# Last grouped FFN of a six-layer transformer kernel: its tokens in three parts, rows sent one token tile per round, some shared-expert work placed between the expert tiles

## The chip, the cores and the metric

The kernel runs on one core of one Trainium2 chip. The metric is device microseconds of one execution, lower is better; a profile of one execution shows where the time goes. The engines are named as in the profile: PE (matrix products; PEld is its weight load), DVE (vector), ACT (scalar), POOL (GpSimd, which also issues the indirect DMAs that scatter and gather rows), SP (which issues the plain DMAs).

## The reference

A residual stream x of 8 x 512 = 4096 tokens by 256 goes through six layers. Only the last one is rebuilt by the change, and its form is that of the fourth:

```python
x = x + 0.5 * _L0_ffn_ref(_layernorm(x), ...)      # 8 experts, expert picks tokens
x = x + _L0_attn_ref(_layernorm(x), ...)           # 16 heads of 16
x = x + 0.5 * _L0_ffn_ref(_layernorm(x), ...)
x = x + 0.5 * _L1_ffn_ref(_layernorm(x), ...)      # grouped FFN, first time
x = x + _L1_attn_ref(_layernorm(x), ...)           # 16 heads of 64
x = x + 0.5 * _L1_ffn_ref(_layernorm(x), ...)      # grouped FFN, last time

def _L1_ffn_ref(x, gate_w, w1, w2, w3, ws1, ws2, ws3):
    scores = softmax(xt @ gate_w.T)                # 16 experts in 4 groups
    # best 2 groups by their largest score, then the best 4 experts in them
    h1 = einsum('td,edi->tei', xt, w1); h3 = einsum('td,edi->tei', xt, w3)
    y = einsum('tei,eid,te->td', silu(h1) * h3, w2, c)   # c: the 4 weights, else 0
    z = silu(xt @ ws1) * (xt @ ws3) @ ws2                # shared expert, all tokens
    return y + z
```

All of it is in float32. A token tile is 128 tokens; there are 32 of them (TT), four to a group (QT).

## The kernel before

**How the grouped FFN is computed** (class Grouped, L1324). Each token goes to 4 of 16 experts. `routing` (L1401) computes for a part of the tokens which experts they choose and, from a running count, at which row of a list of slots each of the four copies belongs. `send` (L1380) scatters the normalised row of one token tile to its four slots in DRAM (`slots_d`): four indirect DMAs of 128 rows each, issued by POOL, at most four in flight. The list has 144 slot tiles of 128 rows, each belonging to one expert. `tile_steps` (L1758) then runs a software pipeline over the slot tiles: in `step(i)` the tile i is transposed (`turn`, tile names tpx, xT), tile i-1 goes through the expert's first products and the silu (`hide`, hs, sgs, as), tile i-3 is turned back (`back`, tpa, aT), and tile i-4 goes through the second product (`give`, yps) and, up to four tiles at a time, to DRAM (`ys_d`). `load` fetches up to four slot tiles (xs) and waits for all sends of the parts up to its own. `collect` (L1593) brings the results back: `gather` (L1562) is one indirect DMA by POOL (yg, 8 buffers), and two token tiles later `add` (L1585) multiplies by the weight and adds into x on DVE. The shared expert is cut into units (`shared`, L1712): per group of four token tiles two "hidden" units (8 products each, tile names hp, sg, at) and four "outputs" units (two products each, yp). `Pump` (L1864) runs such units, each one's DVE part after the next one's PE part.

**Parts.** The tokens are sent in parts so that slot tiles that are already full can be computed before all tokens are routed. `Grouped.__init__` works out which slot tiles are certainly full after each part (`closed`) and after how many tiles in the order of computing a part's results can be gathered (`ready`). The first grouped FFN has parts of (8, 8, 8, 8) token tiles, the last one (20, 12). For (20, 12) this gives closed = 0, 65 and ready = 96, 144.

**The first grouped FFN** (`ffn1_before`, L1889) routes and sends one part after another; `route_and_send` (L1701) has the routing call a function at its end that issues all sends of the part at once.

**The attention ahead of the last FFN** (`_attn1`, L1036) has 64 rounds n (8 sequences by 8 chunks of two heads), each in two halves g. `Front` (L1953) does for the 20 token tiles of part 0 the layer norm, the logits (`units`) and the routing during the attention, and sends them one tile per half in the last 20 halves, with a normalisation of one tile on POOL ahead of each four sends.

**The last grouped FFN** (`ffn1_after`, L2009) loads weights, prepares and routes part 1 (12 tiles), and then runs 148 rounds of `step(i)`. Each round advances the routing of part 1 by two pieces; the routing hands out its 48 sends at once in round 14. From round `begin` = 96 + 6 = 102 on, each round issues one or two gathers. After the loop all 48 shared units are pumped, with the rest of the gathers between them; `done` stores a token tile when both its last expert row and its shared output are added.

**What sets the order.** The code is emitted under a manual schedule, so each engine runs its instructions in the order in which the functions above are called; waits come from data and buffers, and from the dependencies that `send`, `gather` and `load` add by hand. POOL's queue in the last FFN holds only the 48 sends and then the 128 gathers; SP's holds weight loads, xs loads, ys stores and the stores of the output.

Of the kernel before, what the change touches and what calls it, by code (L numbers as in the profile page):

```python
# [9 lines left out]
F32 = mybir.dt.float32  # L10
# [51 lines left out]
class Kernel:  # L62
# [973 lines left out]
    def _attn1(self, ctx, weights, beside, after):  # L1036
# [171 lines left out]

        known = []
        steps = after.routing(0, front.lg, front.pool, row_psum, lambda: known.append(True))  # L1210
        groups = after.parts[0] // QT

# [5 lines left out]
        for first, tiles, n in ((3 * QT, 2 * QT, 10), (5 * QT, 3 * QT, 25)):  # L1218
            for t in range(0, tiles, 2):
                own[n] = moments(pool, stats, first + t)  # L1220
                n += 1
            own[n] = lambda first=first, tiles=tiles: self.ln_finish(pool, stats, first, tiles)

        begin = NC * groups + 2
        for t in range(0, after.parts[0], 2):
            own[33 + t // 2] = moments(front.pool, after.stats, t)
        assert len(own) == 4 + 6 + 2 + after.parts[0] // 2 and max(own) == begin
        last = own[begin]
        own[begin] = lambda: (last(), self.ln_finish(front.pool, after.stats, 0, after.parts[0]))

        E = mybir.EngineType
        with tc.manual_schedule(engines={E.PE, E.DVE, E.Activation, E.Pool}):
# [9 lines left out]
            for n in range(N):  # L1242
                b, c = divmod(n, NC)
                if c == 0:
                    coming = prepare(b + 1) if b + 1 < B else [[]] * NC
                if n + 2 < N:
                    fill += heads(n + 2)
                fill += coming[c]
                if 1 <= n - begin <= groups:
                    fill += front.units(n - begin - 1, row_psum)  # L1250

                def rest():

                    if beside:
                        beside.pop(0)()

                def ahead():

                    if n > begin + groups:
                        advance(steps, 1)  # L1260

                for half in range(2):
                    g = 2 * n + half
                    if g + 1 < 2 * N:
                        exps, divide = scores(g + 1)
                    if half == 0 and tail:
                        tail.pop(0)()
                    t = g - 2 * N + after.parts[0]
                    if t >= 0:
                        assert known  # L1270
                        front.send(t)
                    turn(n, 2 * half)
                    more = g + 1 < 2 * N
                    if more:
                        exps(1)
                    if half == 0 and tail:
                        tail.pop(0)()
                    ahead()
                    if fill:
                        fill.pop(0)()  # L1280
                    if more:
                        divide(0)
                    rest()
                    turn(n, 2 * half + 1)
                    ahead()
                    for _ in range(len(fill) if half else max(0, len(fill) - 3) // 2):
                        fill.pop(0)()
                    if more:
                        divide(1)
                    rest()  # L1290
                    ahead()
                if n in own:
                    own[n]()
                tail = products(n)
                if b > 0 and c < 2:
                    fill += project(b - 1)[2 * c : 2 * c + 2]
# [27 lines left out]
class Grouped:  # L1324
# [6 lines left out]
    def __init__(self, k, n, parts):  # L1331
# [40 lines left out]
        self.stored = []  # L1372

    def rows(self, engine, out, t):
        mv, rstd = self.stats
        engine.tensor_scalar(
            out, self.k.x[:, t, :], mv[:, t, 0:1], rstd[:, t : t + 1], ALU.subtract, ALU.mult
        )

    def send(self, h, t, row):  # L1380

# [3 lines left out]
        for r in range(TOPK):  # L1385
# [10 lines left out]
            tc.declare_no_dep(inst, group=f"read{self.n}", reason="rows of other tiles")  # L1396
            tc.add_to_no_dep_group(f"slots{self.n}", inst)
            self.sent.append(inst)
            self.of_part[h].append(inst)
# [208 lines left out]
    def enter(self, ctx):  # L1608
# [3 lines left out]
        self.work = ctx.enter_context(tc.tile_pool(name=f"f1w_{n}", bufs=2, reuse_waits="tile"))  # L1612
        self.route = ctx.enter_context(tc.tile_pool(name=f"f1r_{n}", bufs=1, reuse_waits="tile"))
        self.psum = ctx.enter_context(tc.tile_pool(name=f"f1p_{n}", bufs=1, space=PSUM, reuse_waits="tile"))
# [56 lines left out]
    def back(self, g):  # L1671
# [6 lines left out]
        if h not in self.lg:  # L1678
            self.lg[h] = self.route.tile([P, self.parts[h], E1], F32, name="lg", bufs=2)
        at = g * QT - self.base[h]  # L1680
        nc.vector.tensor_copy(self.lg[h][:, at : at + QT, :], lg)

    def prepare(self, h):
# [3 lines left out]
        for t in range(a, b, 2):  # L1687
            k.ln_moments(self.route, self.stats, t, 2)
            yield
        k.ln_finish(self.route, self.stats, a, b - a)  # L1690
        yield
# [8 lines left out]

    def route_and_send(self, h):  # L1701
        def send():
            for t in range(self.parts[h]):
                self.send(h, t, self.xn[:, self.base[h] + t, :])

        return self.routing(h, self.lg[h], self.route, self.row_psum, send)

# [4 lines left out]
    def shared(self, g):  # L1712
# [4 lines left out]
        def hidden(s):  # L1717
# [15 lines left out]
            def dve():  # L1733
                at = self.acts[g, s] = self.work.tile([P, CH], F32, name="at", bufs=4)
                nc.vector.tensor_tensor(at, hs[2], hs[1], ALU.mult)
            return pe, dve

        def outputs(i):
# [12 lines left out]
            def dve():  # L1751
                nc.vector.scalar_tensor_tensor(x[:, t, :], box[0], 0.5, x[:, t, :], ALU.mult, ALU.add)
            return pe, dve
# [4 lines left out]
    def tile_steps(self):  # L1758
# [46 lines left out]
        def hide(j):  # L1805
# [9 lines left out]
            st[j]["a"] = work.tile([P, P], F32, name="as", bufs=4)  # L1815
            nc.vector.tensor_tensor(st[j]["a"], sg, hp[:, 1, :], ALU.mult)  # L1816

# [71 lines left out]
def ffn1_before(k, f):  # L1889
# [4 lines left out]
    with ExitStack() as ctx, k.tc.manual_schedule(engines={E.PE, E.DVE, E.Activation, E.Pool, E.SP}):  # L1894
# [13 lines left out]
        for h in range(2):  # L1908

            pair = groups[2 * h : 2 * h + 2]  # L1910
            pump.feed(pair[0][0] + pair[1][0] + pair[0][1] + pair[1][1])
            routing, preparing, more = f.route_and_send(h), f.prepare(h + 1), True
            while more:

                sent = bool(f.of_part[h])
                more = advance(routing, 3)
                if sent:
                    more = advance(preparing, 2) or more
                pump.run(1)
        pump.flush()  # L1920
        load(0)
        for h in (2, 3):
            one, two = groups[2 * h], groups[2 * h + 1]
            pump.feed(one[0] + two[0] + one[1] + two[1])
            routing, preparing, more = f.route_and_send(h), f.prepare(3) if h == 2 else iter(()), True
            while at < f.closed[h - 1] or more:
# [6 lines left out]
                more = advance(preparing, 1) or more  # L1933
                pump.flush()
        while pump.units or pump.pending:
            pump.run(1)
# [16 lines left out]
class Front:  # L1953


    def __init__(self, k, f, ctx):
# [3 lines left out]
        k.nc.sync.dma_start(out=self.gw, in_=k.w["gate_wT"].rearrange("(c p) e -> p c e", p=P))  # L1960
        self.lg = self.pool.tile([P, f.parts[0], E1], F32, name="chosen")
        self.xn = {}
# [8 lines left out]

    def units(self, g, row_psum):

        k, nc = self.k, self.k.nc
        xn = self.normal(g * QT, QT)
        xnT = self.pool.tile([P, DC, CH], F32, name="xnT")
# [19 lines left out]
        def back():  # L1996
            lg = row_psum(QT * E1).rearrange("p (t e) -> p t e", e=E1)
            for i in range(QT):
                nc.tensor.transpose(lg[:, i, :], box[0][:, i * P : i * P + P], k.ident[0:E1, 0:E1])
            nc.vector.tensor_copy(self.lg[:, g * QT : g * QT + QT, :], lg)  # L2000

        box = []
        return [column(c) for c in range(DC)] + [logits, back]

    def send(self, t):
        self.f.send(0, t, self.normal(t, 1)[:, t % QT, :])


def ffn1_after(k, f, out):  # L2009
# [4 lines left out]
    with ExitStack() as ctx, k.tc.manual_schedule(engines={E.PE, E.DVE, E.Activation, E.Pool, E.SP}):  # L2014
        f.enter(ctx)
        a = f.parts[0]
        load, step, total = f.tile_steps()
        f.expert_weights()
        load(0)
        f.shared_weights()  # L2020
        part = f.prepare(1)
        while advance(part, 1):
            pass
        part = f.route_and_send(1)
        left = {t: 2 for t in range(TT)}
# [6 lines left out]
        coming = f.collect(done)  # L2032
        begin = f.ready[0] + 6
        rest, more = list(range(a // QT)), True
        for i in range(total):
            step(i)
            more = more and advance(part, 2)
            if not more and rest and i % 4 == 0:
                f.normal(rest.pop(0))
            if i >= begin:  # L2040
                for _ in range(1 + i % 2):
                    coming.pop(0)()

# [16 lines left out]
        for one, two in zip(groups, groups[1:]):  # L2060
            pump.feed(two[0] + one[1])
        pump.feed(groups[-1][1])
        at = 0
        while pump.units or pump.pending:
            pump.run(1)
# [8 lines left out]
def tile_kernel(tc, w, out):  # L2074
    with ExitStack() as ctx:
# [12 lines left out]
        weights, coming = ffn1_before(k, one)  # L2088
        two = Grouped(k, 1, (20, 12))
        k.attn1(weights, coming, two)  # L2090
# [74 lines left out]
```

## Time and profile before

| | us |
|---|---|
| median of 3 runs (4102.02 to 4124.71) | 4116.74 |
| the profiled execution | 4112.13 |
| its span, first to last instruction | 4110.4 |
| ... first grouped FFN, about | 1847 to 2373 |
| ... attention ahead of the last FFN, about | 2383 to 3627 |
| ... last grouped FFN | 3627 to 4110 |
| PE busy, of the span | 3641.7 (89%) |
| DVE / ACT / POOL busy | 2113.4 / 1475.7 / 1204.1 |

The profile is one execution. Windows of the span show for each engine how long it was busy and at what share of full speed PE's clock was granted. A timeline line gives start, duration, engine, line, operation, and in brackets how long the engine sat idle before it and who ended that; "remote" and "another core or an unknown queue" stand where the profile finds no releaser, "issue" where the engine waited for nothing that the profile shows. An indirect DMA's line shows the time that POOL spends on issuing it, not its transfer.

### The profile page before, as it was taken

The page shows a single profiled execution, that of the slowest core. Times are in us where ns is not written, and L with a number is a line of the kernel's source. Part 1 is how long each engine was busy: PE and PEld are TensorE (multiplying, and loading weights), DVE is VectorE, ACT ScalarE, POOL GpSimd, SP SyncE. Part 2 cuts the span into 40 slices and gives each one's busy share as a digit, 9 for nine tenths or more (in the row PEclk, how much of TensorE's full clock was granted, in tenths as well). Part 3 has the DMA queues.
Part 4 walks back from the last instruction along what each step waited for, and adds up shares of the span by engine and source line. Part 5 has one row for each costly group of instructions (what it writes and reads, how often), then busy time and mean ns, then how long its engine had stood idle before and what let it go on. Part 6 is the DMA issues. An engine that isn't in the chain of part 4 may idle for free.

```text
span 4110.4 us, 51131 instructions
## 1 busy us (share of the span) xinstructions
PE 3641.7 (89%) x17088; PEld 2139.1 (52%) x17088; DVE 2113.4 (51%) x5628; ACT 1475.7 (36%) x3387; POOL 1204.1 (29%) x1098
## 2 busy tenths in 40 slices
PE   4999979999995799986668989999999999986978
PEld 2666643444442566653346844555555444554754
DVE  6222126666665321214432578777777678652354
ACT  3222223444443222221224435445444434432421
POOL 2433333433412333323351512200000205513165
PEclk7999987999987899997788999999999999987998
DMA  5333247311003233324134711000000001143453
GB/s 194 68 78 74 57 108 241 114 27 27 14 19 104 55 67 71 80 51 134 58 131 147 250 31 32 27 10 1 1 1 1 1 1 48 56 147 127 158 168 105
DMA packets 262994, 316.62 MB, mean 77 GB/s; under 512 B 31697, under 2 KB 232785, under 8 KB 262481
## 3 DMA queue, kind: packets, MB, share of 16 engines
q1 hardware_dynamic: 213584, 212.12, 16.2%
q0 software_dynamic: 49152, 101.24, 10.1%
q8 instruction: 142, 2.33, 0.2%
q14 instruction: 116, 0.94, 0.1%
HBM read 157.81 MB, written 147.06 MB: 74 GB/s over the span
## 4 chain that ended last, share of the span: by engine, by line
PE 52%; issue 11%; DVE 8%; POOL 4%; another core or an unknown queue 4%; ACT 3%; DMA 1%; POOLq 0%; ACTq 0%; DVEq 0%
PE hs L1808 6%; PE zp L1175 5%; PE sp L1127 5%; PE tp L1161 5%; PE pq L1102 4%; PE yps L1828 3%; PE yp L1194 3%; PE pv L1082 3%; PE hp L1724 3%; PE st L874 3%; POOL acc_d L538 2%; PE sp L833 2%; PE tpx L1790 2%; PE pp L726 2%
## 5 line engine op out<-in xcount | busy, mean ns | idle before, releaser
L1139 ACT ACTIVATE ex<-sp,nmax 128x512 f32<-128x512 f32 x512 | 344.8, 685 | 469.5 <-DVE nmax L1132 454.9
L531 PE MATMUL op<-w,hid 128*128 128x256 f32 x2048 | 456.2, 380 | 0.0
L518 PE MATMUL hp<-exT,w 128*128 128x512 f32 x1024 | 450.1, 598 | 0.0
L1568 POOL DMA_INDIRECT yg<-ys_d,slot x256 | 266.4, 1040 | 573.6 <-DMA ys_d<-ys 210.4
L531 PEld LDWEIGHTS op<-w,hid 128*128 128x128 f32 x2048 | 384.9, 190 | 57.0 <-issue 7.7
L538 POOL DMA_INDIRECT acc_d<-ob,idx x128 | 207.0, 1617 | 571.9 <-ACT ob L537 571.9
L1808 PE MATMUL hs<-w_sb,xT 128*128 (+1 forms) x1152 | 321.7, 404 | 50.9 <-ACT xT L1792 25.7
L536 DVE TENSOR_TENSOR ob<-op,b 128x256 f32<-128x256 f32 x128 | 54.4, 425 | 542.8 <-PE op L531 465.7
L1161 PEld LDWEIGHTS tp<-ident,ex 128*128 128x128 f32 x2048 | 228.7, 141 | 182.6 <-issue 107.7
L518 PEld LDWEIGHTS hp<-exT,w 128*128 128x128 f32 x1024 | 193.9, 192 | 233.1 <-issue 231.8
L1132 DVE TENSOR_REDUCE nmax<-sp 128x2 f32<-128x1024 f32 x256 | 300.3, 1214 | 17.5 <-PE sp L1127 16.2
L522 ACT ACTIVATE hid<-hp,b 128x512 f32<-128x512 f32 x256 | 175.9, 687 | 324.1 <-PE hp L518 304.5
L841 DVE CUSTOM_DVE_ANT_0 junk<-sp,mask 128x256 f32<-128x256 f32 (+3 forms) x512 | 249.5, 487 | 81.6 <-PE sp L833 58.4
L1161 PE MATMUL tp<-ident,ex 128*128 128x128 f32 x2048 | 279.3, 279 | 13.5 <-DVE eT L204 12.5
L1386 POOL DMA_INDIRECT slots_d<-wide,slot x176 | 173.8, 988 | 337.7 <-DVE lane L1523 231.7
L1127 PE MATMUL sp<-qk,qk 64*128 64x512 f32 x1024 | 257.4, 621 | 2.2 <-ACT ex L1139 2.2
L1808 PEld LDWEIGHTS hs<-w_sb,xT 128*128 128x128 f32 x1152 | 209.2, 202 | 80.2 <-ACT xT L1792 30.4
L1149 DVE TENSOR_SCALAR ex<-ex,rec 128x512 f32<-128x512 f32 x512 | 245.7, 522 | 8.8
L1102 PE MATMUL pq<-xnT,wide 128*128 128x512 f32 x512 | 241.7, 596 | 5.5 <-ACT qk L1108 5.5
L1816 DVE TENSOR_TENSOR as<-sgs,hs 128x128 f32<-128x128 f32 x288 | 82.4, 286 | 303.9 <-ACT sgs L1814 245.1
L1175 PE MATMUL zp<-eT,v 128*64 128x512 f32 x1024 | 234.9, 599 | 0.0
L889 ACT ACTIVATE ex<-st 128x768 f32<-128x768 f32 (+1 forms) x192 | 168.5, 882 | 160.1 <-DVE st L887 157.4
(346 smaller groups left out, 5740.7 us busy)
## 6 DMA issues: line engine op xcount, KB each, us to landing
xs<-slots_d SPq DMA_DIRECT2D x70, 512.0 KB
ys_d<-ys SPq DMA_DIRECT2D x70, 512.0 KB
w<-in_W SPq DMA_DIRECT2D x32, 1024.0 KB
slots_d<-mask SPq DMA_DIRECT2D x8, 2304.0 KB
ys_d<-mask SPq DMA_DIRECT2D x8, 2304.0 KB
w_sb<-in_w SPq DMA_DIRECT2D x24, 512.0 KB
xn_d<-xn SPq DMA_DIRECT2D x16, 512.0 KB
acc_d<-x SPq DMA_DIRECT2D x8, 1024.0 KB
```

What stands on the lines that cost most here:

```text
L518: nc.tensor.matmul(hp, lhsT=w1[:, c, f * P : f * P + P], rhs=exT[e][:, c, h * CH : h * CH + CH], start=(c == 0), stop=(c == DC - 1),)
L531: nc.tensor.matmul(op, lhsT=hid[h][:, f, i * P : i * P + P], rhs=w2[:, f, :], start=(f == 0), stop=(f == FC - 1),)
L538: inst = nc.gpsimd.indirect_dma_start(out=acc_d[:, :], out_offset=bass.IndirectOffsetOnAxis(ap=idx[:, e, st : st + 1], axis=0), in_=ob, in ...
L841: nc.vector.tensor_tensor_reduce(out=junk[:, :wd], in0=sps[h // 2][:, h % 2, at : at + wd], in1=mask[:, S - wd :], scale=1.0, scalar=NEG, ...
L1102: nc.tensor.matmul(pp, lhsT=(wq, wk)[a][:, k, c * P : c * P + P], rhs=seq[b]["xnT"][:, k, :], start=(k == 0), stop=(k == DC - 1),)
L1127: nc.tensor.matmul(sp[:, j, :], lhsT=q[r, qt * P : qt * P + P], rhs=k[r, :], start=True, stop=True)
L1132: nc.vector.tensor_reduce(m, sp, AX.X, ALU.max, negate=True)
L1139: nc.scalar.activation(ch["ex", 2 * half + i][:, j, :], sps[i][:, j, :], AF.Exp, bias=nmax[i][:, j : j + 1], accum_out=sums[i][:, j : j + 1],)
L1161: nc.tensor.transpose(tp[:, k, :], ch["ex", qt][:, j, k * P : k * P + P], self.ident)
L1175: nc.tensor.matmul(zp[DK1 * j : DK1 * j + DK1, :], lhsT=seq[b]["v", h][:, k, at : at + DK1], rhs=ch["eT"][:, j, k, :], start=(k == 0), sto ...
L1568: inst = nc.gpsimd.indirect_dma_start(out=self.y[t, r], out_offset=None, in_=self.k.ys_d[:, :], in_offset=bass.IndirectOffsetOnAxis(ap=sel ...
L1808: nc.tensor.matmul(hp.rearrange("p a i -> p (a i)"), lhsT=st[j]["xT"][:, c, :], rhs=self.w13[:, st[j]["e"], c, :].rearrange("p e i -> p (e ...
```

## The change

The last FFN has the parts (12, 8, 12) instead of (20, 12). By the same arithmetic closed = 0, 33, 49 and ready = 65, 112, 144; the number of xs loads and ys stores stays 37 each.

In the attention, `Front` keeps logits for two parts and runs two routings: part 0 (12 tiles) is ready at round 26, part 1 (8 tiles) at round 42. Part 0 is sent in halves 96 to 107, part 1 in halves 112 to 119 (before: 108 to 127). The pieces of the layer norm are spread over the rounds in which the rows become final.

`route_and_send` becomes `route`, which puts a part's tiles in a list, and `send_next`, which sends one tile from it. `send` gets an argument `behind`: the first of a tile's four DMAs waits for the DVE instruction last recorded in `self.latest` (a product of a slot tile or of the shared expert). Both grouped FFNs use it: the first one once per round of its loops (which go on until the list is empty), the last one in every odd round.

In `ffn1_after` the routing of the last part advances by three pieces per round, so that it hands out its tiles in round 9; 14 of the 48 shared units (6 hidden, 8 outputs, of the last part's tokens) run in rounds 32 to 45, one per round with its DVE part at once; gathers begin in round 71 for part 0 (48 of them), in round 118 for part 1 (32), and after the loop for part 2 (48). With more than two parts `give` (unchanged) lets ACT instead of DVE copy the results of the slot tiles below closed[-1], here the first 49.

```diff
@@ _attn1
-        steps = after.routing(0, front.lg, front.pool, row_psum, lambda: known.append(True))
-        groups = after.parts[0] // QT
+        known, steps = {}, {}
+        ahead_of = [(h, NC * after.base[h + 1] // QT + 2) for h in range(len(after.parts) - 1)]
+        sends = {}
+        for h, begin in ahead_of:
+            steps[h] = after.routing(h, front.lg[h], front.pool, row_psum, lambda h=h: known.setdefault(h, True))
+        at = 2 * N - 4
+        for h, _ in reversed(ahead_of):
+            at -= after.parts[h] + 4
+            for t in range(after.parts[h]):
+                sends[at + t] = (h, t)
...
-        for t in range(0, after.parts[0], 2):
-            own[33 + t // 2] = moments(front.pool, after.stats, t)
+        for h, begin in ahead_of:
+            first, tiles = after.base[h], after.parts[h]
+            for t in range(first, first + tiles, 2):
+                n = NC * (t // QT + 1) + 2
+                own.setdefault(min(n + 1 + t % QT, begin), []).append(moments(front.pool, after.stats, t))
...
-                if 1 <= n - begin <= groups:
-                    fill += front.units(n - begin - 1, row_psum)
+                for h, begin in ahead_of:
+                    if 1 <= n - begin <= after.parts[h] // QT:
+                        fill += front.units(h, n - begin - 1, row_psum)
...
-                    if n > begin + groups:
-                        advance(steps, 1)
+                    for h, begin in ahead_of:
+                        if n > begin + after.parts[h] // QT:
+                            advance(steps[h], 1)
...
-                    t = g - 2 * N + after.parts[0]
-                    if t >= 0:
-                        assert known
-                        front.send(t)
+                    if g in sends:
+                        h, t = sends[g]
+                        assert h in known
+                        front.send(h, t)
@@ Grouped
+            if behind is not None and r == 0:
+                tc.add_manual_dep(inst, behind.name, SYNC, reason="rows go at the pace of the products")
...
-    def route_and_send(self, h):
-        def send():
-            for t in range(self.parts[h]):
-                self.send(h, t, self.xn[:, self.base[h] + t, :])
-
-        return self.routing(h, self.lg[h], self.route, self.row_psum, send)
+    def route(self, h):
+        return self.routing(
+            h, self.lg[h], self.rpool, self.row_psum,
+            lambda: self.waiting.extend((h, t) for t in range(self.parts[h])),
+        )
+
+    def send_next(self):
+        if self.waiting:
+            h, t = self.waiting.pop(0)
+            self.send(h, t, self.xn[:, self.base[h] + t, :], self.latest)
+        return bool(self.waiting)
...
-            nc.vector.tensor_tensor(st[j]["a"], sg, hp[:, 1, :], ALU.mult)
+            self.latest = nc.vector.tensor_tensor(st[j]["a"], sg, hp[:, 1, :], ALU.mult).ins
@@ ffn1_before
-                sent = bool(f.of_part[h])
+                sent = bool(f.waiting or f.of_part[h])
                 more = advance(routing, 3)
                 if sent:
                     more = advance(preparing, 2) or more
                 pump.run(1)
+                more = f.send_next() or more
...
                 pump.flush()
+                more = f.send_next() or more
@@ ffn1_after
-        part = f.prepare(1)
+        part = f.prepare(last)
...
-        begin = f.ready[0] + 6
         rest, more = list(range(a // QT)), True
-        for i in range(total):
-            step(i)
-            more = more and advance(part, 2)
-            if not more and rest and i % 4 == 0:
-                f.normal(rest.pop(0))
-            if i >= begin:
-                for _ in range(1 + i % 2):
-                    coming.pop(0)()
+
+        def begin():
+            t = (TT + 2) - -(-len(coming) // TOPK)
+            return f.ready[sum(t >= b for b in f.base[1:-1])] + 6
...
+        early = 6 * ((TT - a) // QT) - 4
         at = 0
+        for i in range(total):
+            step(i)
+            if f.closed[last] - 3 - early <= i < f.closed[last] - 3:
+                pump.run(1)
+                pump.flush()
+                at += 1
+            more = more and advance(part, 3)
+            if i % 2:
+                f.send_next()
+            if not more and not f.waiting and rest and i % 4 == 0:
+                f.normal(rest.pop(0))
+            for _ in range(1 + i % 2):
+                if i >= begin():
+                    coming.pop(0)()
         while pump.units or pump.pending:
             pump.run(1)
@@ tile_kernel
-        two = Grouped(k, 1, (20, 12))
+        two = Grouped(k, 1, (12, 8, 12))
```

## The prediction

> **What bounds the kernel now.** I read the busy tenths first: PE is at 9 almost everywhere, with the lows in the two grouped FFNs. Windows of 20 us of the last one, then the timeline of the lowest windows, show why.
>
> ```profile
> core 0: us, PE busy (x) PEld busy (x) DVE busy (x) ACT busy (x) POOL busy (x), PEclk, DMA share, GB/s
> 3680.00:3700.00 20.00, 13.41 (x50) 9.29 (x50) 8.35 (x29) 3.86 (x13) 13.97 (x15) 0.73 0.57 190
> 3700.00:3720.00 20.00, 6.96 (x17) 4.19 (x18) 1.00 (x3) 1.35 (x5) 15.43 (x16) 0.50 0.29 105
> 3720.00:3740.00 20.00, 2.62 (x7) 1.31 (x5) 0.42 (x1) 0.37 (x1) 15.12 (x17) 0.50 0.27 98
> ...
> 3760.00:3780.00 20.00, 20.00 (x112) 16.91 (x111) 10.50 (x33) 9.96 (x37) 0.00 (x0) 1.00 0.53 171
> 3440.00:3560.00 120.00, 116.87 (x532) 62.21 (x534) 85.28 (x162) 53.81 (x136) 91.43 (x84) 0.97 0.21 74
> 2240.00:2360.00 120.00, 114.24 (x601) 93.77 (x600) 65.92 (x189) 53.29 (x200) 65.33 (x64) 0.97 0.78 250
> 3895.00:3985.00 90.00, 75.75 (x351) 57.67 (x350) 50.68 (x139) 30.66 (x115) 58.30 (x57) 0.93 0.59 181
> 3985.00:4091.00 106.00, 83.35 (x246) 45.74 (x244) 45.18 (x102) 12.85 (x22) 67.97 (x66) 0.87 0.38 110
> ```
>
> From 3700 to 3740 PE, DVE and ACT all nearly stop while POOL issues the 48 sends of the last part, one per 1.29 us (0.98 busy, 0.30 between); 20 us later PE is full. The timeline of that stretch (start, duration, engine, ...):
>
> ```profile
> 3716.55 0.98 POOL L1386 DMA_INDIRECT slots_d<-wide,slot  x1 [0.30 <-issue]
> 3729.72 0.37 ACT L1792 COPY xT<-tpx 128x256 f32<-128x256 f32 x1 [10.99 <-remote]
> 3730.15 2.07 PE L1808 MATMUL hs<-w_sb,xT 128*128 x4 [9.61 <-issue]
> 3740.17 0.28 ACT L1814 ACTIVATE sgs<-hs 128x128 f32<-128x128 f32 x1 [10.07 <-remote]
> ```
>
> ACT starts its copies and silus up to 11 us after the one before, with no releaser in sight; PE follows at once. The stall begins some 12 us after the first send (3680.66) and is gone after the last (3743.3). The other windows say when it comes. Sends in the attention (3440 to 3560, four of them and then a normalisation on POOL, one DMA per 1.8 us) leave PE at 97%; so do gathers at one per round of the first FFN (2240 to 2360, one per 1.9 us). Gathers with up to two per round (3895 to 3985, one per 1.58 us, PE 84%) and those between the shared units (3985 to 4091, one per 1.61, PE 79%) hurt. So what hurts is POOL issuing indirect DMAs without a pause, not their number. Why, the profile doesn't say.
>
> **What the Trainium skill says.** Perfetto Trace Analysis, "DMA Instruction — SWDGE (GPSIMD)": the time shown for such a DMA is that of writing its descriptors, not of its transfer. The trace agrees: 0.98 us each, and the next one is let go 0.30 us later. TensorE: Matmul & The Clock Gate, "Part 1: The HAM clock gate": an idle PE runs at half clock. It agrees: 0.50 in the windows above, so a stall also makes the work in it dearer. SBUF — State Buffer, "SBUF: two separate sides", has only DVE and GpSimd share a port pair and ACT wait for nobody; it doesn't explain why ACT is late here, so I price the stall by the trace alone.
>
> **The change part by part.** Sums are against the profiled execution, 4112.13 us (span 4110.40), which is 4.6 below the median of 4116.74. A clean round of the slot-tile loop takes 1.63 us (hs at 3761.46 and 3763.09 in the chain); all 148 would be 241 us.
>
> 1. *First send earlier.* Before, the routing runs on DVE from 3643.24 to 3680.6, DVE about 90% busy, with 14 rounds between: 16 products `as` of 0.28 and 14 copies `ys` of 0.42, together 10.4 us. Now it needs 9 rounds, and `ys` is ACT's: 2.5 us. First send 8 us earlier, 3673. ACT gets 0.37 us more per round, 1.28 in all of 1.63; from 2180 to 2200 it does the same beside a full PE (20.00). No cost.
>
> 2. *Sends, one tile per two rounds.* Two clean rounds are 3.3 us, four sends 5.2, so POOL falls behind and issues without a pause until the engines stall; then POOL runs out of released tiles, pauses, and they recover. The 12th tile is released in round 31. If POOL is the limit, 48 x 1.29 = 62 us, 9% more for its pauses (in their loop the gathers took 100 / 69 = 1.45 us each where back to back they take 1.33, 1.02 and 0.31), 67 us: last four sends from 3735, which is when round 31 has run. Before, round 25 runs at 3749.07 and round 31 at 3758.9. Gain 24 us. If nothing stalls, round 31 is at 3673 + 22 x 1.63 = 3709: gain 50. POOL's pauses should let the engines do a little better than POOL's limit; I take 27. Below nothing is possible, see the last rival. Behind the waiting send stand only the other sends; who waits for those is the xs load ahead of round 49, reached some 50 us after round 31: covered.
>
> 3. *14 shared units moved to rounds 32 to 45.* Hidden 3.57 (7.13 for two), outputs 0.9 (3.57 for four): 6 x 3.57 + 8 x 0.9 = 28.6 us of PE, put where PE is full at 1.63 a round. Cost 28.6; at best some of it falls into stalls of late sends (0 to 5).
>
> 4. *Tail.* Before, from 3983.9 to 4107.1, 123 us. A set of two hidden and four outputs units took 16.3 (4011.39 to 4093.06, five sets) with ten gathers in it. Left now: five sets and four outputs, 48 gathers instead of 59: 5 x 16.3 + 3.6 = 85, and 3 for the wait of the first gather for the last store (0 to 6). Gain 35.
>
> 5. *Gathers in the loop.* Before, 69 gathers lie in rounds 102 to 147, 100 us where 46 x 1.63 = 75 would do: 0.36 us lost per gather. Now 80: +4 (0 to 8).
>
> 6. *One more border between parts*, where the next xs load can't be issued a group ahead: the one at 3816.16 costs 4.14. +4.
>
> 7. *Attention.* Five groups of logits cost 4.9 us each as before. One routing of 20 tiles cost 10 us (zp from 3384.20 to 3445.60 is 61.4 us, where the undisturbed cycle has 51.4). Two of 12 and 8 have the same elements, but the small DVE instructions twice, some 40 x 0.17 = 7 us, on a DVE 71% busy. +3 (0 to +8). Sends earlier by 8 to 12 halves: their cover, PE at 97%, stays.
>
> 8. *First FFN.* Its tiles are released one per round, but a round there takes 2 to 4 us of DVE or is a short outputs unit, so 8 tiles are free within some 15 us, where POOL has sent three. The stall comes after 12 us all the same. In its last part some hidden units move into rounds whose DVE work leaves PE idle: -2 (-8 to +5).
>
> Sum: -27 + 28.6 - 35 + 4 + 4 + 3 - 2 = -24. **Forecast 4116.74 - 24 = 4092 us**; with the bounds of its own terms 4080 to 4106.
>
> **The rivals.**
> *A: no stall.* Four sends at a time don't stall the attention, so paced sends may not stall here. Gain 50 instead of 27, and the early units hide part of the sends: -47, 4069. Against: two rounds are shorter than four sends, so there is no pause until something is late.
> *B: given back.* The gathers take 128 x 1.61 = 206 us with their stalls and start at round 71. By items 2, 3 and 6 that is 3840; two pauses of POOL (rounds 103 to 117, 24 us, and 139 to the tail, 18) and 6 us of last outputs give 4094 for an end at 4107. With the attention at +8: -5, 4112. For: POOL's spacing is worst just there.
> *C: slower.* The wait of the sends on DVE works against itself: DVE is held up by the stall, each tile waits for two stalled rounds, and round 31, behind it round 49, come late. Stalled rounds took 5.7 us (hs at 3694.11 and 3699.84), so 11.4 per tile, round 31 at 3673 + 11 x 11.4 = 3798, 39 later than before instead of 27 earlier: +42, 4158. It decides from 7.6 us per tile (break-even of the whole) and is 0.5% slower from 9.4. Against: at 3749 the engines ran at full pace within a few us of POOL's pause.
>
> **How the numbers follow.** Forecast 0.47, A 0.20, B 0.22, C 0.11. Measurement tells about 0.5% from no change, 20.6 us, so faster is below 4096.2. Of the forecast's range some 0.6 lies below that (0.28), with A 0.20 and a little of B (0.03): 0.51 faster. Same: the rest of the forecast (0.19), of B (0.19), a little of C (0.02): 0.40. Slower 0.09. The range, 4062 to 4124, takes in A and B and leaves out C and the far end of A.
>
> **What would show it.** First send near 3673 and the last tile's sends 62 to 70 us later, with gaps ahead of groups of four; PE well above the 6.96 and 2.62 of 20 there; hs of rounds 32 to 45 spaced by 1.63 plus a unit; a tail of about 88 us; attention longer by 0 to 8; the first FFN within 8 us of before. The forecast is wrong if the sends take over 90 us, if round 49 waits for xs, or if the gathers' part of the loop loses more than 0.5 us per gather.

## The result and the profile after

The changed kernel takes 4095.62 us (median of 14 runs) where the kernel before takes 4116.76 beside it. The ratio is 0.9955, 95% interval 0.9943 to 0.9968: by it the kernel is 18 us faster, 0.45%, just inside what the prediction had called no change; the two medians lie 21 us apart. One of the 14 runs of the kernel before took 6673.92 us, and the ratio leaves it out. The profiled execution took 4101.16 us, span 4099.4. It lies 5.5 above its median and the one of before 4.6 below its own, so the two profiles differ by only 11 us. Sums of stages, which can only be read from the profiles, add up to those 11 and not to the 18 or 21.

The windows of the last FFN in the changed kernel (busy us of each engine, granted clock, DMA share, GB/s):

```profile
3660.00:3680.00 20.00, 10.19 (x42) 7.42 (x41) 14.67 (x56) 4.56 (x16) 1.96 (x2) 0.82 0.18 59
3680.00:3700.00 20.00, 15.54 (x66) 11.91 (x64) 4.08 (x10) 7.07 (x26) 13.73 (x14) 0.84 0.58 196
3700.00:3720.00 20.00, 13.35 (x54) 10.08 (x54) 1.44 (x5) 6.65 (x23) 11.78 (x12) 0.74 0.41 134
3720.00:3740.00 20.00, 13.45 (x51) 9.77 (x52) 1.99 (x7) 7.07 (x28) 11.78 (x12) 0.77 0.41 145
3740.00:3760.00 20.00, 18.13 (x61) 11.19 (x61) 4.12 (x12) 7.03 (x23) 7.85 (x8) 0.89 0.49 158
3760.00:3840.00 80.00, 79.87 (x395) 62.21 (x394) 28.19 (x82) 37.88 (x131) 0.04 (x1) 1.00 0.37 119
3840.00:3920.00 80.00, 67.10 (x313) 51.41 (x312) 39.84 (x110) 27.92 (x105) 49.81 (x48) 0.91 0.60 190
...
4020.00:4040.00 20.00, 9.56 (x33) 5.61 (x32) 6.02 (x14) 1.77 (x3) 13.26 (x13) 0.78 0.48 138
```

PE, which had 6.96 and 2.62 of 20 us during the sends, has 13 to 15.5 now: half of the hole is filled, not all (from the first send to the silu numbered 45 below, PE idles 20.0 us instead of 43.7). From 3760 to 3840, with nothing on POOL, PE is full and takes the shared units between its rounds. With the gathers (3840) it loses again, 12.9 us in 80. The timeline of the first stall (start, duration, engine, line, what, idle before) shows a pause at work:

```profile
3686.61 0.98 POOL L1402 DMA_INDIRECT slots_d<-wide,slot  x1 [0.30 <-issue]
3689.07 0.28 ACT L1841 ACTIVATE sgs<-hs 128x128 f32<-128x128 f32 x1 [3.14 <-remote]
3689.38 0.29 DVE L1843 TENSOR_TENSOR as<-sgs,hs 128x128 f32<-128x128 f32 x1 [5.08 <-ACT sgs L1841]
3689.94 0.98 POOL L1402 DMA_INDIRECT slots_d<-wide,slot  x1 [2.35 <-DVE as L1843]
...
3698.94 0.98 POOL L1402 DMA_INDIRECT slots_d<-wide,slot  x1 [0.31 <-DMA slots_d<-wide,slot]
3699.27 0.28 ACT L1841 ACTIVATE sgs<-hs 128x128 f32<-128x128 f32 x1 [3.16 <-PE hs L1835]
```

The sends begin at 3677.61. The send at 3686.61 is the eighth without a pause; ACT and DVE have then sat idle for 3 and 5 us, the sends of the next tile wait for DVE's product `as`, so POOL pauses 2.35 us, and ACT goes on 2.5 us after the last send began. Then come the next eight, and the next stall.

To compare stages I take the 144 silus `sgs` on ACT, one for each slot tile, numbered from 0, as marks of how far the loop has come; a clean round is 1.63 us, so 72 of them 117.4.

| us, from the profiles | before | after |
|---|---|---|
| last `yp` of the attention starts | 3626.8 | 3628.5 |
| first, last send of the last part | 3680.7, 3742.3 | 3677.6, 3750.3 |
| silu 31 | 3764.0 | 3746.0 |
| silu 31 to 45 (with 14 units in the changed kernel) | 22.8 | 53.0 |
| 45 to 71 | 49.2 | 42.6 |
| 71 to 143 | 145.5 | 157.5 |
| 143 to the end of the span | 128.9 | 100.2 |

### The profile page after: what moved, and what is told of

Same layout as the page of the kernel before. It is cut to its first block, busy times and chain, and to the rows that moved or that the text cites. A ratio compares the mean times of both kernels' runs of the same rounds, so it can differ in the third digit from the quotient of the medians.

```text
span 4099.4 us, 51269 instructions
## 1 busy us (share of the span) xinstructions
PE 3645.5 (89%) x17094; PEld 2136.2 (52%) x17094; DVE 2109.9 (51%) x5683; ACT 1492.8 (36%) x3440; POOL 1202.2 (29%) x1098
## 4 chain that ended last, share of the span: by engine, by line
PE 64%; issue 14%; DVE 10%; POOL 4%; ACT 4%; another core or an unknown queue 2%; DMA 2%; SPq 0%; POOLq 0%; ACTq 0%; DVEq 0%
PE hs L1835 6%; PE op L531 5%; PE hp L518 5%; PE zp L1175 5%; PE sp L1127 5%; PE pq L1102 4%; PE tp L1161 4%; PE yps L1855 3%; PE pv L1082 3%; PE hp L1749 3%; PE st L874 2%; PE yp L1194 2%; POOL acc_d L538 2%; PE pp L726 2%; PE sp L833 2%
## 5 line engine op out<-in xcount | busy, mean ns | idle before, releaser
L1132 DVE TENSOR_REDUCE nmax<-sp 128x2 f32<-128x1024 f32 x256 | 300.5, 1215 | 13.7 <-PE sp L1127 13.7
L1843 DVE TENSOR_TENSOR as<-sgs,hs 128x128 f32<-128x128 f32 x288 | 82.5, 287 | 326.8 <-ACT sgs L1841 255.6
```

The costliest lines, as they stand in the source:

```text
L1132: nc.vector.tensor_reduce(m, sp, AX.X, ALU.max, negate=True)
```

## The experiments

Each is an edit of the changed kernel, and each ratio is to the kernel before on the same chip; 0.9955 is the changed kernel's own. The interval behind a ratio is the 95% one. The experiments fell on four chips, and these are of two sorts. On two of them the kernel before takes 4111.3 and 4117.5 us, as in the case itself; on the other two 3911.6 and 3913.9. I call them the slow and the fast chips; they turned out to be the main finding. Each chip was used in one session only, so the record can't tell a property of the chip from one of the time.

**Sends without pace (slow chip).**

```diff
-            if i % 2:
-                f.send_next()
+            while f.waiting:
+                h, t = f.waiting.pop(0)
+                f.send(h, t, f.xn[:, f.base[h] + t, :])
```

> The changed kernel with the sends of its last part issued in one go as soon as the slots are known, without waits on DVE (the first FFN's sends stay paced). My theory: the engines stall while POOL issues without a pause, so one burst from about 3678 to 3741 stops PE as before; the silu with index 31 (counted from the loop's first) came 83.3 us after the first send in the kernel before and 68.4 in the changed one, so this kernel loses about 15 us against the changed one: ratio to the kernel before near 0.999, PE below 4 of 20 us at the end of the burst. Rival (the gain comes from the earlier first send, the parts and the early units alone): ratio 0.9955 as the changed one, within 0.001. Rival C (waiting on DVE costs): below 0.994.

Ratio 1.0023 (1.0011 to 1.0034): 0.0068, or 28 us, slower than the changed kernel, and slower than before. Its windows:

```profile
3700.00:3720.00 20.00, 5.41 (x13) 2.92 (x12) 0.29 (x1) 1.29 (x4) 15.12 (x17) 0.50 0.28 99
3720.00:3740.00 20.00, 3.83 (x9) 2.24 (x9) 0.29 (x1) 1.29 (x4) 15.35 (x16) 0.50 0.47 158
```

The hole is back: four ACT instructions in 20 us. The ratio is worse than the 0.999 expected, and away from both rivals. From the first send to silu 31 it takes 95.1 us against 68.4, so the pacing by itself is worth 27 us here. My 83.3 was wrong for this kernel: six more rounds are left to run when its sends begin (silu 9 was done, not 15), and 6 x 1.63 = 9.8. Without the pacing the change is a small loss here, not a gain.

**No shared units between slot tiles (slow chip).** `early = 0`.

> The changed kernel with no shared units between the slot tiles (all 34 + 14 in the tail). My theory: the 14 units cost 30 us in the loop and take as much out of the tail, so nothing but their place changes; the number of gathers in the loop stays 80 and the tail has 48 gathers for 14 more units, so POOL leaves the engines more pauses there: ratio 0.994 to 0.996. Rival (they fill stalls or hide late sends): 0.9985 or more, with PE idle or an xs wait ahead of round 49.

Ratio 0.9957 (0.9941 to 0.9973), equal to the changed kernel's. From the first send to silu 45 it takes 23 us less (98.5), and the tail 9 more (109.2). The 14 us between them are of the size of what one execution says: the profiled one lies 6.8 us below its median, the changed kernel's 5.5 above. By the ratio, as expected, where the units stand doesn't matter within what these runs can tell.

**The same units among the sends (slow chip).**

```diff
-            if f.closed[last] - 3 - early <= i < f.closed[last] - 3:
+            if 10 <= i < 10 + early:
```

> The changed kernel with the 14 early shared units in rounds 10 to 23 instead of 32 to 45, so that seven of the twelve tiles are sent beside longer rounds. PE idles 19.8 us between 3677 and 3750 in the changed kernel. My theory: a round of 1.63 + 2.04 us leaves POOL a pause ahead of each tile, and a unit's few long instructions need ACT and DVE seldom, so 10 to 15 us of that are won: ratio 0.992 to 0.993. Rival (the stall hits long instructions as well, or the last sends come late and xs with them): 0.9955 or more.

Ratio 0.9935 (0.9913 to 0.9957); first send to silu 45 takes 107.7 us instead of 121.4. These 13.7 us are the size that the theory gave (10 to 15). But PE's idle time fell by 4 us only, from 20.0 to 15.9; the rest goes with a higher granted clock, 0.94 over the sends instead of 0.80. The ratio lies between the theory's 0.992 to 0.993 and the rival's 0.9955, and its interval holds both, so it decides nothing. PE has 67.41 busy of the 81 us of the sends, where it had 53.20 of 73.

**One gather per round (slow chip, twice).**

```diff
-            for _ in range(1 + i % 2):
+            for _ in range(1):
```

> The changed kernel with one gather per round of the loop instead of one and two in turn. In the changed kernel 80 gathers lie in the loop, which from round 71 on loses some 0.5 us for each. My theory: one gather of 1.29 us per round of 1.63 leaves POOL a pause each round, the loop loses at most 0.2 us per gather, and nearly as many fit (77): about 25 us shorter, ratio 0.988 to 0.991. Rival (the loss is one per gather however it is spaced, or the gathers only move to the tail): 0.9945 or more.

Ratio 0.9894 (0.9873 to 0.9914), and on the other slow chip 0.9885 (0.9866 to 0.9904), both as expected. The windows over its rounds 71 to 143, and over those of the changed kernel:

```profile
3847.00:3967.00 120.00, 118.41 (x647) 98.86 (x645) 72.74 (x209) 57.62 (x215) 72.30 (x71) 1.00 0.71 225
```

```profile
3842.00:3999.00 157.00, 135.14 (x644) 105.22 (x643) 77.52 (x216) 57.07 (x214) 81.36 (x79) 0.92 0.57 179
```

71 gathers and 647 products in 120 us with PE full, against 79 and 644 in 157. Silu 71 to 143 takes 120.2 us where 72 clean rounds take 117.4: one gather in a round of 1.63 us costs nearly nothing (2.8 us in 72 rounds); up to two in a round cost 40 us. It is not the number of gathers, 71 against 79. The gathers that are left don't pile up much in the tail: it is 102.4 us long, and 106.6 on the other chip, instead of 100.2. The changed kernel shows the same within itself: from 3916.3 to 3942.2 POOL issues nothing, as the gathers of the next part may start only in round 118, and there the silus 105 to 119 follow each other at 1.63 us.

**Bursts in the attention (fast chip).** Four tiles' rows are normalised on POOL and their 16 sends issued in a row, every fourth half.

```diff
-                        front.send(h, t)
+                        if t % QT == QT - 1:
+                            front.send_four(h, t - 3)
...
```

> The changed kernel with the attention's sends issued four tiles at a time: four normalisations on POOL and then 16 sends in a row, once in every four halves, instead of one of each four in every half. My theory (POOL without a pause stalls any engine that works beside it): five bursts of 21 us, stalled from 8 to 12 us after their start, cost 20 to 40 us; PE falls below 70% in the second half of each; ratio 1.000 or more. Rival (only stages with many short instructions are stalled; the attention's matmuls of 512 columns are not): PE stays at 93% or more beside the bursts, ratio 0.9955 within 0.0015.

Ratio 1.0035 (1.0024 to 1.0047), with the kernel before at 3911.6. The bursts cost nothing: from the first `pv` to the last `yp` the attention takes 1244.2 us, and 1245.0 in a kernel without bursts on that chip (the next one). But on this chip nothing stalls beside the sends of the last part either (first send to silu 31 takes 38.7 us), so for the slow chips the question stays open.

**Three more on the fast chip,** all with one gather per round. The first moves the tail's gathers:

```diff
-            for _ in range(min((3, 3, 1, 1, 1, 1)[at % 6], len(coming))):
+            for _ in range(min((1, 1, 3, 3, 1, 1)[at % 6], len(coming))):
```

> gather_one with the tail's gathers moved against the units: three beside each of the long hidden units and one beside each outputs unit, instead of three beside two of the outputs units. Theory (in the tail POOL and DVE wait for each other, since adds stand behind a product that waits for PE): more even, 3 to 8 us shorter, ratio 0.9875 to 0.9887. Rival (the tail is the last part's 48 gathers at POOL's own pace): 0.9894 within 0.001.

Ratio 1.0002 (0.9993 to 1.0012). The second also has `early = 0`:

> gather_one with no shared units between the slot tiles. Theory: the tail is bound by the gathers of the last part (12 us from the loop's last product to the last store, 48 gathers at 1.7 us, 8 us of ending: about 100 us) and PE has only 57 us of units there, so 14 more (28.6 us) cost nothing in it, while the loop is 30 us shorter: ratio 0.982 to 0.984. Rival (PE with its stalls bounds the tail, as with no_early, which gained nothing): 0.988 or more.

Ratio 1.0000 (0.9992 to 1.0009): the tail is 100.0 us instead of 82.5, the first send to silu 45 70.6 instead of 91.2. The third sends slower and spreads the units:

```diff
-            if f.closed[last] - 3 - early <= i < f.closed[last] - 3:
+            if 10 <= i < 10 + 2 * early and i % 2 == 0:
...
-            if i % 2:
+            if i % 3 == 0:
                 f.send_next()
```

> gather_one with a tile sent every third round instead of every second and the 14 early units spread over the even rounds 10 to 36: a tile of four sends (5.2 us of POOL) then has 7.8 us of rounds. Theory (pauses of POOL cure the stall): from the first send to the silu with index 45 some 90 us instead of 121.5, PE idle below 6 us there instead of 20; ratio 0.981 to 0.984. Rival (the loss is one per send, however they are spaced): PE idle of 15 to 20 us, 0.987 or more.

Ratio 1.0004 (0.9995 to 1.0013). All three expectations were written for a stall that wasn't there, so they decide nothing about it. That three so different orders give the same time as before says that on this chip none of them has much to win.

**The changed kernel on a fast chip, and the slow sends beside it.**

> The changed kernel itself once more, since the last four kernels ran where the kernel before takes 3911.6 us instead of 4111 and no stall is seen beside the sends. If the kernel before takes about 4110 here: 0.9955 within 0.001 again. If it takes about 3911: the sends cost nothing in either kernel, the pacing and the early units win nothing, and the gathers at one and two per round make adds wait on DVE for their landing (23.5 us in the kernel with bursts in the attention, whose ratio was 1.0035): theory 1.002 to 1.005. Rival (the parts win their part of the tail all the same): 0.998 or less.

> The kernel with one gather per round, a tile sent every third round and 14 units spread over the rounds of the sends, beside the changed kernel. Where the stall is (kernel before about 4110): first send to the silu with index 45 some 90 us instead of 121.5, ratio 0.981 to 0.984; rival (one loss per send however spaced) 0.987 or more. Where it is not (about 3911): 1.000 as before, since nothing is there to be won.

Ratios 1.0036 (1.0022 to 1.0050) and 1.0003 (0.9996 to 1.0010), both as expected for a chip without the stall. Here the change makes the kernel slower by 0.36%. Two windows of the changed kernel there, the second over all of its sends, then its timeline on POOL, and the same stretch on ACT:

```profile
3600.00:3620.00 20.00, 20.00 (x111) 16.82 (x111) 3.46 (x12) 13.23 (x50) 14.71 (x15) 1.00 0.63 212
...
3580.00:3645.00 65.00, 61.14 (x268) 44.52 (x269) 15.25 (x47) 30.79 (x107) 45.83 (x47) 0.93 0.61 201
```

```profile
3614.89 0.98 POOL L1402 DMA_INDIRECT slots_d<-wide,slot  x1 [0.30 <-issue]
3616.17 0.98 POOL L1402 DMA_INDIRECT slots_d<-wide,slot  x1 [0.30 <-DMA slots_d<-wide,slot]
3617.46 0.98 POOL L1402 DMA_INDIRECT slots_d<-wide,slot  x1 [0.30 <-issue]
```

```profile
3616.47 0.28 ACT L1841 ACTIVATE sgs<-hs 128x128 f32<-128x128 f32 x1 [0.44 <-PE hs L1835]
3618.10 0.28 ACT L1841 ACTIVATE sgs<-hs 128x128 f32<-128x128 f32 x1 [0.44 <-PE hs L1835]
```

POOL issues at the very same pace, 0.98 busy and 0.30 between, and ACT is on time, one silu per 1.63 us. Silu 15 to 31 takes 26.3 us, 16 clean rounds. What hurts the changed kernel here is something else. DVE's waits in the loop, in the changed kernel (3718 to 3845) and then in the one with one gather per round and slow sends (3725 to 3843):

```profile
DVE as L1843 <- ACT sgs L1841: 27.1, 35, 1.2
DVE x L1605 <- DMA yg<-ys_d,slot: 24.2, 22, 2.6
```

```profile
DVE as L1843 <- ACT sgs L1841: 43.4, 70, 1.4
```

With up to two gathers per round the adds (`x`) reach DVE before their rows have landed and hold up the `as` behind them: silu 71 to 143 takes 128.0 us instead of 118.3. The other fast chip agrees: in the kernel with bursts, which has up to two gathers per round, DVE waits 23.5 us for rows and this stage takes 130.5 us; in the next one, with one gather, 117.8. Their medians are 12.2 us apart, those of the first pair 10.8. That the rest of the kernels makes no difference is likely from this, not shown: one gather per round alone never ran on a fast chip.

On the slow chip it is not this wait. DVE's idle time ahead of the adds (last figure ahead of any arrow) in the same stage of the changed kernel, on the slow chip and then on the fast one:

```profile
L1605 DVE SCALAR_TENSOR_TENSOR x<-yg,coef,x 128x256 f32<-128x256 f32 x72 | 34.0, 478 | 0.6
```

```profile
L1605 DVE SCALAR_TENSOR_TENSOR x<-yg,coef,x 128x256 f32<-128x256 f32 x72 | 34.4, 482 | 24.8 <-DMA yg<-ys_d,slot 24.2
```

There DVE idles 68.2 us ahead of `as` instead, 52.2 of them put down to ACT's silu, and ACT comes up to 3.9 us late: it looks like the stall beside the sends.

**One gather per round, and slow sends with it (slow chip).**

> One gather per round of the loop, alone, once more. Where the kernel before takes about 4110: 0.9894 within 0.002, as before. Where it takes about 3911: theory (the changed kernel's 1.0036 there comes from adds that wait on DVE for gathers at one and two per round): 1.000 within 0.001, DVE's wait for the landing of yg in the loop below 3 us. Rival (it comes from the attention, the parts or the early units): 1.003 or more.

> The same with a tile sent every third round and 14 units spread over the rounds of the sends. Where the kernel before takes about 4110: theory (pauses of POOL cure the stall) 0.981 to 0.984, PE idle below 6 us between the first send and the silu with index 45; rival (one loss per send however spaced) 0.987 or more. Where it takes about 3911: 1.000 within 0.001, nothing to be won.

Ratios 0.9885 (0.9866 to 0.9904) and 0.9831 (0.9812 to 0.9849). The window over the sends of the second:

```profile
3683.00:3783.00 100.00, 89.57 (x399) 65.91 (x399) 21.93 (x63) 42.53 (x148) 47.10 (x48) 0.95 0.45 150
```

First send to silu 45 takes 99.6 us instead of the changed kernel's 121.4, PE idles 10.4 us of them instead of 20. The ratio came as expected. The idle time did not fall below 6 as expected; 3.9 us of it are one wait for xs at 3749.58, for slot tile 33, the first behind a border between parts. (The last tile is sent at 3779.9, just ahead of round 49, but PE waits only 0.6 us there.) The same 48 sends, spaced out, cost half: the rival of one loss per send falls. The spacing comes from two edits at once, the third round and the units among the sends; with the units alone PE idled 15.9 us, so what each does is not told apart. This kernel beats both: 4047.6 us on a slow chip against 4117.5 before, and the time of before on a fast one, where the changed kernel is 0.36% slower.

## Why the prediction held, point by point

The time came 3.6 us from the forecast, and that close it came in part by luck. Summed over the stages the profiles show 11 us where the forecast had 24; that the medians differ by 21 is due to where the two profiled executions lie among the others. Among the steps are errors of both signs. By its steps, from the profiles:

1. *First send 8 us earlier: mis-sized.* It came 3.1 earlier, after an attention that ended 1.7 later, so 4.8. The routing is DVE's. Ahead of the first send the trace of before has 14 `as` and 11 `ys` on DVE, 8.5 us, where the prediction counted 16 and 14, 10.4 us; and DVE was busy for 30.1 of its 37.4 us, 80% and not 90. From the last `yp` to the first send DVE's busy time fell from 36.9 to 32.1 us, and that is the whole gain.
2. *27 us from the pacing: right in kind, short in size.* Silu 31 is 18 us earlier (20 with the attention's end taken off). The sends took 72.7 us from first to last, not 67, since four pauses of 2.1 to 4.1 us and three short ones came on top of POOL's 62. Against one burst at the same place the pacing is worth 27.
3. *28.6 for the early units: right.* Silu 31 to 45 takes 30.2 longer. In the kernel with all sends at once, where the sends are over by then, it takes 51.6, 28.8 above the 22.8 of before.
4. *Tail 35 shorter: 28.7.* PE falls to 9.56 of 20 in the stalls that are left there (4020 to 4040).
5. *Gathers in the loop, 0.36 us each: too low.* Silu 71 to 143 takes 12 us more than before, not 4, and 40 above 72 clean rounds: 0.50 per gather for 80, which is just where the prediction would have called itself wrong. The step took the mean loss of before as a price per gather. The runs show no such price: one gather per round loses 2.8 us in 72 rounds. On the slow chip the loss is a stall that comes with up to two per round, and there DVE does not wait for the rows; on the fast chips it does, and that costs some 10 us.
6. *Another border, 4 us: wrong.* The wait of 3.72 us for an xs load now falls at 3745.98, inside the stage of the sends, and 45 to 71 is 6.6 us shorter than before, as the old border at 3816.16 is gone from there. The wait moved; none was added, and round 49 doesn't wait for xs.
7. *Attention +3: +4.3.* (1242.0 to 1246.3; 1244 to 1249 in the four kernels that share its code and ran beside each other.)
8. *First FFN -2: -2.5 in the profile, but not settled.* It ended between 2379 and 2391, and lasted 521 to 528 us, in those four kernels with the same code in it, so a few us can't be read from one execution. Pacing its sends was not tried apart, nor the three parts alone.

Sum: -2.5 + 4.3 - 19.7 + 30.2 - 6.6 + 12.0 - 28.7 = -11.0, the difference of the two spans. One reading of the prediction was off without bearing on the sum: beside the first FFN's gathers (2240 to 2360) PE has 114.24 of 120 us, 95% and not 97.

Of the rivals, *A* (no stall) is wrong on the slow chips, where the case's times were taken. On the fast chips the stall is absent, and the gain with it. *B* (given back by gathers) was the direction of the error: 8 us more in the loop and 6 less out of the tail. *C* (the wait works against itself) is excluded: without the wait the kernel is 28 us slower.

The premise that carried it, that POOL issuing without a pause hurts and not the number of DMAs, is shown on the slow chips from both sides, by the sends (one burst, every second round, every third) and by the gathers. Every edit spaces both the issuing on POOL and the transfers that it starts, so which of the two hurts is not told apart. What the prediction couldn't know from one profile is that the stall comes on some chips, or at some times, only.

## What to carry to other kernels

Where a stall shows only as engines that start late with no releaser, look at what another engine does without a pause, and space it out: one gather per 1.63 us round cost nearly nothing here, three in two rounds cost 40 us in 72 rounds. Here the rate mattered more than the place: the changed kernel paced its sends and left its gathers at one and two in turn, and the gathers alone held more (25 us) than the whole change won. A gain that comes out of such a stall should be measured on more than one chip before it is kept.

## What was not expected of the hardware

The same kernel before takes 4111 to 4117 us on some chips and 3912 to 3914 on others. The changed kernel, of which there is a trace on both sorts, shows that all of the difference lies in the two grouped FFNs, where POOL issues indirect DMAs beside the slot tiles: the first takes 524.9 and 422.6 us, the last one from the last `yp` to the end 470.9 and 393.0. The first grouped FFN, before the change on a slow chip and after it on a fast one:

```profile
1857.00:2384.00 527.00, 391.39 (x1681) 276.33 (x1682) 238.67 (x847) 169.23 (x537) 192.39 (x193) 0.85 0.42 139
```

```profile
1863.00:2288.00 425.00, 372.29 (x1684) 268.06 (x1684) 240.35 (x847) 169.23 (x537) 194.48 (x193) 0.93 0.51 170
```

The same work, 193 indirect DMAs or normalisations of POOL among it, 105 us apart (527.3 and 422.6 us from the first `hp` to the attention's first `pv`). One tile per round has done little there on the slow chip; what stalls it there was not looked into. The attention takes 1242 to 1250 us over all traces of both sorts. A page of the Trainium skill that I had named, SBUF — State Buffer ("SBUF: two separate sides"), has DMA and the engines apart in SBUF; the fast chips agree (15 sends in 20 us beside 20.00 us of PE), and on the slow ones it says nothing of why ACT starts its copies and silus up to 11 us after the one before.

Slower transfers don't explain the difference. The packets of the two large DMA queues (packets, MB, share of 16 engines), on the slow chip and then on the fast one:

```profile
q1 hardware_dynamic: 213584, 212.12, 16.2%
q0 software_dynamic: 49152, 101.24, 10.1%
```

```profile
q1 hardware_dynamic: 213584, 212.12, 16.9%
q0 software_dynamic: 49152, 101.24, 10.5%
```

Of spans of 4099.4 and 3924.8 us these shares are 664 and 414 us, and 663 and 412: the same time for the same packets.

One more difference can be seen: the list of DMA issues gives the median time to landing on a fast chip, and can't on a slow one, whose trace lacks many of the landings. The changed kernel on a slow chip, then on a fast one:

```profile
yg<-ys_d,slot POOLq DMA_INDIRECT x256
slots_d<-wide,slot POOLq DMA_INDIRECT x176
```

```profile
yg<-ys_d,slot POOLq DMA_INDIRECT x256, 3.3
slots_d<-wide,slot POOLq DMA_INDIRECT x176, 2.4
```

Whether what delays ACT and DVE there also loses the records, and what it is, stays open. Every execution on record here has a span and a clock from such records, so even whether the recording takes part in the stall is not known.
